# A graph layer in fp32: the convolution's weights as a ring of nine single taps, more lead in the first group, fewer turns of the identity

## The chip, the cores and the metric

The kernel runs on one core of a Trainium2 chip. The metric is the device time of one execution in microseconds; three executions of the kernel before are given with their median. The profile is that of one more execution, taken by the hardware profiler. The engines are TensorE (PE: matmuls; PEld: its weight loads, which lie beside them), VectorE (DVE), ScalarE (ACT), GpSimd (POOL) and SyncE (SP, which issues most of the DMAs).

## The reference, cut to what matters

Inputs: `x` (32, 512, 256) and a 0/1 matrix `adj` (32, 512, 512), all in fp32, with the weights of one layer. Cut down, the reference is

```python
h = maximum(layernorm(x), 0)
# 1: two convolutions along the 512 positions, 1 tap and 17 taps, 256 -> 256 channels
c = relu(bn1(conv1d(h, conv1_w)))
x_conv = relu(bn2(conv1d(c, conv2_w, pad=8)) + h)
# 2: messages over the graph
s = h @ w_se.T + b_se                                  # 3 numbers a node
A = exp(-squared_distance(s, s)) * adj
x_nmp = A @ relu(h @ w_msg.T + b_msg)
# 3: a gated unit
gi = concat(x_conv, x_nmp) @ w_ih.T + b_ih
gh = h @ w_hh.T + b_hh
r, z = sigmoid(gi_r + gh_r), sigmoid(gi_z + gh_z)
n = tanh(gi_n + r * gh_n)
out = x + (1 - z) * n + z * h
```

## The kernel before, in words

**The 17-tap convolution** is the part that the change touches. It is done by a fast algorithm with two nested levels of five evaluation points: 25 products of transformed weights with transformed inputs take the place of the direct sum of taps. The 32 batches are laid end to end and cut into 7 groups (`STARTS`, L36), since one group's input is what the memory holds. So there are 7 x 25 = 175 products, numbered m = 25 g + n. Each product has an operand `x2` (made on VectorE from the first convolution's output `h1`, by `fives`, `operands` and `operand_some`, L432 to L492 and L741) and a weight `w` with two or three parts, here called taps, of `[128, 2, 256]` each (index k of `w[:, k]`, L524). A product with n = 6 (`LONE`) uses tap 1 alone.

In the **first group** (g = 0) the weights are made on the chip: `weights_first` (L527) combines rows of `wraw` on VectorE into `gg`, ScalarE scales them into `w` (two activations of 512 columns, L558) and issues one DMA that puts both taps into DRAM (`WD`, L562). `prepare_some` (L757) runs this generator piece by piece, never further than three weights beyond the product in work. A product of this group is two halves on TensorE, each of 16 matmul instructions of 116 columns, which read taps 0 and 1.

From the **second group** on the weights are read back: `weights_again` (L567) takes a buffer and issues one DMA on SP for all taps of one product. In the second group tap 2 is the sum of taps 0 and 1, made on VectorE (`third_weight`, L577) and also put into DRAM; later groups read all three. A product then is: tap 2 with `x2[1]` into PSUM, a copy of the result by ScalarE, then taps 0 and 1 with the differences `xd` (L843 to L849). Weights have 3 buffers of three taps, `x2` has 6 buffers. `AHEAD` (L726) limits how many operands are made beyond the product in work: one more than its value.

**The order of all work is planned by the program itself** when it is built. Five streams (rows, begins, graphs, conv, gates; L1336) are Python generators. A planner (L1383) holds a clock `now` of TensorE's time, made of estimates for each instruction (`matmul`, `turn`, and the `Engine` class for VectorE and ScalarE), and at each turn of its loop lets the stream that is furthest behind its share emit its next piece. Every engine works its own instructions strictly in the order in which they were emitted. Where a stream yields a time, it isn't asked again before that time; where it yields a function, it waits until that is true. Between the pieces `fill` and `background` (L1260) emit VectorE's and ScalarE's work that nobody waits for yet: layer norms, operands, weights, sums; weights and operands of the next two products go first.

If no stream is ready, the planner adds 0.25 us to `now` and tries again (L1386). From the third such round in a row on it emits, on each round, **two turns of the identity** on TensorE (`keep_warm`, L143): transposes into a PSUM tile that nobody reads (`unused`, named `ps_acc`). They don't move `now`. This ends as soon as the first gate's input is asked for (`HB`), which is after all 25 weights are made, near the end of the first group. Another 16 such turns stand at the start (L1349).

`load_graph` (tile `hTg`), `load_gates` (`hTb`), `load_sums` (`xnb`) and the masks (`m_sb`, in `Graphs.ask`) are DMAs on SP's queue, as are the weights that are read back; `hT` and `x_sb` are loaded there too.

Of the kernel before, what the change touches and what calls it, by code (L numbers as in the profile page):

```python
# [49 lines left out]
def kernel(  # L50
# [434 lines left out]
    def operands(g):  # L485

        rv = sizes(g)[3]
        h = h1[:, : Q * rv].rearrange("p (q e) -> p q e", q=Q)
        for x1 in fives(h, 6, rv, lambda: phases("x1", 6, rv, 2), again=True):
            yield None  # L490
            if x1 is not None:
                yield from fives(x1, 2, rv, lambda: phases("x2", 2, rv, 6))  # L492
# [30 lines left out]

    def new_w():  # L524
        return cv.tile([P, 3, ND, D], F32, name="w", bufs=3)

    def weights_first():  # L527
# [10 lines left out]
        for j1 in ORDER:  # L538
# [12 lines left out]
            for j2 in ORDER:  # L551
# [5 lines left out]
                w = new_w()  # L557
                for i in range(ND):  # L558
                    act.activation(
                        w[:, :2, i, :], gg[i], AF.Copy, scale=GSCALE[j1] * GSCALE[j2]  # L560
                    )
                nc.scalar.dma_start(WD[len(WS)][:, :2], w[:, :2])  # L562
# [4 lines left out]
    def weights_again(m):  # L567

        w = new_w()
        k = slice(1, 2) if m % 25 == LONE else slice(0, 2 if m < 50 else 3)  # L570
        nc.sync.dma_start(w[:, k], WD[m % 25][:, k])
        WS.append(w)
        W_AT.append(now + 7.0)
# [3 lines left out]
    def third_weight(m):  # L577
        if m in thirds or m % 25 == LONE:
            return
        thirds.add(m)  # L580
        w = WS[m]
        dve.tensor_tensor(w[:, 2], w[:, 0], w[:, 1], op=ALU.add)
        later(dve.free + 0.4, lambda: nc.gpsimd.dma_start(WD[m % 25][:, 2], w[:, 2]))
        W_AT[m] = dve.free + LAG
# [141 lines left out]
    AHEAD = 3  # L726
# [31 lines left out]
    def prepare_some():  # L758
        nonlocal prepare_at
        if len(WS) >= 25 or len(WS) >= at_product + 3 or now < prepare_at:  # L760
            return False
# [3 lines left out]
    def convolution():  # L765
# [3 lines left out]
        def product(ps, *terms, clear=(True, True)):  # L769


            for o in range(ND):
                pairs = [
                    (w[:, k, i, o * P : (o + 1) * P], t[:, at + i * (nu + 1) : at + i * (nu + 1) + nu])
# [19 lines left out]
        for g in range(NG):  # L794
# [9 lines left out]
            for n in range(25):  # L804
# [3 lines left out]
                while 25 <= len(WS) < min(m + 2, 25 * NG):  # L808
                    weights_again(len(WS))
# [26 lines left out]
                else:  # L836
# [5 lines left out]
                    else:  # L842
# [3 lines left out]
                        if 25 <= len(WS) == m + 2 < 25 * NG:  # L846
                            weights_again(m + 2)
# [8 lines left out]
                if 25 <= len(WS) == m + 2 < 25 * NG:  # L856
                    weights_again(m + 2)
# [525 lines left out]
    while streams:  # L1383
        names = [k for k in streams if hold[k] is None or hold[k]()]
        able = [k for k in names if ready[k] <= now]
        if not able:  # L1386
# [3 lines left out]
            if waits > 2 and not HB:  # L1390
                keep_warm(2)
# [67 lines left out]
```

## Time and profile before

| | us |
|---|---|
| median of three runs | 2068.64 (2067.52 to 2070.0) |
| the profiled execution | 2070.59 |
| its span, first to last instruction | 2068.8 |
| first products of the second convolution start | 57.5 |
| the first group's last product ends | 231.5 |
| first gate matmuls | 247.3 |

The parts of the page used below are the busy time of each engine with its share of the span and its instructions, and the clock granted to TensorE in 40 slices, in tenths of full speed. A table by stretches gives, for each, its length, then the busy time of PE, PEld, DVE, ACT and POOL with the number of instructions, the mean clock, the share of time that the DMA engines were busy, and GB/s. A line of time gives the start and the length of an instruction (or of several alike in a row), engine, line, operation, output and input by name, form and count; in brackets stands the idle time of the engine ahead of it, and what ended it. Nearly all instructions carry the line of the helper that emitted them: L136 (matmul), L141 (turn), L146 (turn of the identity), L127 (VectorE and ScalarE), so one goes by the names of the tiles. In the first group `ps_c<-x,w` are the products of the second convolution, `ps_g<-ident,m_sb` the masks' turns, `ps_g<-at,msg` the sums over the graph, `w<-gg` the scaling of weights, `x<-x` the operands.

### The profile page before, as it was taken

What the parts mean: (1) busy time and instruction counts of PE and PEld (TensorE: products, weight loads), DVE (VectorE), ACT (ScalarE), POOL (GpSimd) and SP (SyncE); (2) the same over time, 40 slices, a digit from 0 to 9 for tenths busy, and PEclk for the clock granted to TensorE, in tenths of its full rate; (3) what the DMA queues carried; (4) which work ended last, traced back from release to release, by engine and by line L of the source; (5) the groups of instructions that cost most, each with busy time, mean ns of one, the idle gap of its engine ahead of it and who ended that gap; (6) DMA issues with size and microseconds to landing.
All of it is one profiled execution on the core that took longest, in us unless ns stands there. A gap on an engine that the chain in (4) does not pass through costs nothing.

```text
span 2068.8 us, 25327 instructions
## 1 busy us (share of the span) xinstructions
PE 2046.3 (99%) x8724; PEld 1256.4 (61%) x8724; DVE 1319.8 (64%) x2378; ACT 827.0 (40%) x1585; POOL 451.7 (22%) x578
## 2 busy tenths in 40 slices
PE   9999999999999999999999999999999999999998
PEld 5888566666666666665666665566665666644444
DVE  5789677865877667775677663667766576532223
ACT  6544553343543446234353333533344433342221
POOL 2101122321312113221132212322211211132222
PEclk9999999999999999999999999999999999999999
DMA  7455768887889768986799876978776777555554
GB/s 274 162 173 194 250 202 224 190 216 200 193 243 208 195 187 227 211 198 177 189 214 219 188 197 155 227 192 193 171 206 176 184 176 158 148 113 91 68 92 36
DMA packets 539312, 378.31 MB, mean 183 GB/s; under 512 B 452992, under 2 KB 470432, under 8 KB 538048
## 3 DMA queue, kind: packets, MB, share of 16 engines
q1 hardware_dynamic: 381312, 278.74, 47.9%
q0 software_dynamic: 153184, 84.70, 23.9%
q10 hardware_dynamic: 4688, 13.24, 1.7%
q8 instruction: 70, 1.15, 0.2%
q14 instruction: 58, 0.48, 0.1%
HBM read 278.55 MB, written 114.56 MB: 190 GB/s over the span
## 4 chain that ended last, share of the span: by engine, by line
PE 61%; DVE 1%; issue 1%; DMA 0%; POOL 0%; ACT 0%; DVEq 0%; POOLq 0%; ACTq 0%
PE ps_acc L136 36%; PE ps_c L136 13%; PE ps_g L136 10%; PE ps_c L917 1%; PE ps_g L141 0%; DMA cd<-part 0%; DVE y L127 0%; POOL cd L721 0%; DVE part L127 0%; ACT part L127 0%; DVE o_sb L127 0%; DVE right L127 0%; DVE x L127 0%; POOL out_dram L1146 0%; PE ps_g L917 0%
## 5 line engine op out<-in xcount | busy, mean ns | idle before, releaser
L1146 POOL DMA_DIRECT2D out_dram<-o_sb x252 | 276.6, 1733 | 522.1 <-DVE o_sb L127 512.6
L136 PE MATMUL ps_acc<-xconv,wih 128*128 128x512 f32 (+1 forms) x772 | 361.3, 590 | 0.0
L136 PE MATMUL ps_acc<-xnb,wih 128*128 128x512 f32 (+1 forms) x772 | 360.4, 592 | 0.0
L136 PE MATMUL ps_acc<-hTb,whh 128*128 128x512 f32 (+1 forms) x772 | 356.1, 590 | 0.0
L136 PEld LDWEIGHTS ps_c<-xd,w 128*128 128x128 f32 x2304 | 288.6, 191 | 65.2 <-issue 56.2
L136 PEld LDWEIGHTS ps_c<-x,w 128*128 128x128 f32 x2032 | 256.1, 191 | 82.9 <-issue 66.2
L136 PE MATMUL ps_c<-xd,w 128*128 128x135 f32 (+1 forms) x2304 | 291.9, 280 | 0.7 <-ACT ps_c L127 0.4
L136 PE MATMUL ps_c<-x,w 128*128 128x135 f32 (+2 forms) x2032 | 265.3, 279 | 3.1 <-ACT n L127 1.7
L136 PE MATMUL ps_g<-at,msg 128*128 128x512 f32 x512 | 227.0, 593 | 1.3 <-DVE at L127 1.3
L136 PEld LDWEIGHTS ps_acc<-xnb,wih 128*128 128x128 f32 x772 | 141.4, 191 | 140.8 <-issue 137.5
L136 PEld LDWEIGHTS ps_acc<-xconv,wih 128*128 128x128 f32 x772 | 140.7, 190 | 141.6 <-issue 139.7
L136 PEld LDWEIGHTS ps_acc<-hTb,whh 128*128 128x128 f32 x772 | 140.5, 190 | 138.9 <-issue 136.9
L127 DVE TENSOR_TENSOR o_sb<-hTb,r 128x512 f32<-128x512 f32 x63 | 43.4, 689 | 215.6 <-ACT r L127 215.5
L127 DVE TENSOR_TENSOR msg<-ps_g,bmsg 128x256 f32<-128x256 f32 x128 | 54.0, 422 | 190.5 <-PE ps_g L136 190.4
L136 PEld LDWEIGHTS ps_g<-at,msg 128*128 128x128 f32 x512 | 95.0, 190 | 109.4 <-issue 103.8
L127 DVE SCALAR_TENSOR_TENSOR x<-x,x 128x544 f32<-128x544 f32 (+5 forms) x161 | 137.6, 854 | 2.7
L127 DVE TENSOR_TENSOR xd<-x 128x544 f32<-128x544 f32 (+1 forms) x144 | 102.5, 717 | 42.4 <-PE ps_c L136 42.3
L127 DVE TENSOR_TENSOR x<-x 128x272 f32<-128x272 f32 (+5 forms) x280 | 127.1, 498 | 0.3
L136 PE MATMUL ps_g<-wmsg,hTg 128*128 128x259 f32 x496 | 122.3, 381 | 0.0
L136 PE MATMUL ps_g<-hT,w 128*128 128x512 f32 (+8 forms) x296 | 117.6, 545 | 0.0
L127 ACT ACTIVATE ps_c<-ps_c 128x270 f32<-128x270 f32 (+1 forms) x144 | 56.6, 393 | 150.6 <-PE ps_c L136 150.5
L127 ACT ACTIVATE z<-ps_acc,brz 128x512 f32<-128x512 f32 x64 | 43.9, 686 | 179.0 <-PE ps_acc L136 179.0
(124 smaller groups left out, 2354.2 us busy)
## 6 DMA issues: line engine op xcount, KB each, us to landing
w<-wd SPq DMA_DIRECT2D x120, 768.0 KB, 5.6
m_sb<-in_adj_dram SPq DMA_DIRECT2D x384, 64.0 KB, 3.9
hT<-hd SPq DMA_DIRECT2D x33, 512.0 KB, 4.4
hd<-hT POOLq DMA_DIRECT2D x32, 512.0 KB, 6.4
hTb<-hd SPq DMA_DIRECT2D x32, 512.0 KB, 5.3
xnb<-nd SPq DMA_DIRECT2D x64, 256.0 KB, 3.1
out_dram<-o_sb POOLq DMA_DIRECT2D x252, 64.0 KB, 5.0
hTg<-hd SPq DMA_DIRECT2D x31, 512.0 KB, 4.5
```

The costliest lines, as they stand in the source:

```text
L127: getattr(self.engine, name)(*tiles, **more)
L136: nc.tensor.matmul(ps, lhsT, rhs, **more)
L917: nc.tensor.matmul(pss[c], gr.left[k, :], gr.right[k, :], start=True, stop=True, tile_position=(32 * c, 0),)
L1146: nc.gpsimd.dma_start(dst, src, accum_op=ALU.add)
```

## The change

Four edits go together.

1. A weight buffer holds one tap instead of three, and there are nine of them instead of three (the same memory). In the first group two taps are taken per product; each is scaled by two activations of 256 columns and put into DRAM by a DMA of its own. In later groups `weights_again` becomes one generator over all products that takes and loads tap by tap, in the order in which the product uses them (2, 0, 1). `load_weights` runs it until nine taps beyond those done are asked for: at the start of a product, and once more behind its first third. The calls at the end of a product are dropped.
2. `AHEAD` is 4 instead of 3, and `x2` has 7 buffers instead of 6.
3. Weights of the first group may be made five beyond the product in work instead of three.
4. While no stream is ready, one turn of the identity is emitted on rounds 3, 7, 11 and so on of the wait, instead of two on each round from the third.

```diff
--- before.py
+++ after.py
@@ -489,7 +489,7 @@
         for x1 in fives(h, 6, rv, lambda: phases("x1", 6, rv, 2), again=True):
             yield None
             if x1 is not None:
-                yield from fives(x1, 2, rv, lambda: phases("x2", 2, rv, 6))
+                yield from fives(x1, 2, rv, lambda: phases("x2", 2, rv, 7))
 
     def ends(x2, rv):
 
@@ -521,8 +521,13 @@
 
     WS, W_AT = [], []
 
+    RING = 9
+    W_BASE, taken = [], 0
+
     def new_w():
-        return cv.tile([P, 3, ND, D], F32, name="w", bufs=3)
+        nonlocal taken
+        taken += 1
+        return cv.tile([P, ND, D], F32, name="w", bufs=RING)
 
     def weights_first():
 
@@ -554,23 +559,38 @@
                     gg.append(next(inner[i]))
                     yield 0.0
                 yield dve.free + 0.1
-                w = new_w()
-                for i in range(ND):
-                    act.activation(
-                        w[:, :2, i, :], gg[i], AF.Copy, scale=GSCALE[j1] * GSCALE[j2]
-                    )
-                nc.scalar.dma_start(WD[len(WS)][:, :2], w[:, :2])
+                W_BASE.append(taken)
+                w = [new_w(), new_w()]
+                for k in range(2):
+                    for i in range(ND):
+                        act.activation(
+                            w[k][:, i, :], gg[i][:, k, :], AF.Copy, scale=GSCALE[j1] * GSCALE[j2]
+                        )
+                    nc.scalar.dma_start(WD[len(WS)][:, k], w[k])
                 WS.append(w)
                 W_AT.append(act.free + LAG)
                 yield 0.0
 
-    def weights_again(m):
-
-        w = new_w()
-        k = slice(1, 2) if m % 25 == LONE else slice(0, 2 if m < 50 else 3)
-        nc.sync.dma_start(w[:, k], WD[m % 25][:, k])
-        WS.append(w)
-        W_AT.append(now + 7.0)
+    def weights_again():
+        for m in range(25, 25 * NG):
+            W_BASE.append(taken)
+            w = {}
+            for k in (1,) if m % 25 == LONE else (2, 0, 1):
+                yield
+                w[k] = new_w()
+                if k < 2 or m >= 50:
+                    nc.sync.dma_start(w[k], WD[m % 25][:, k])
+            WS.append(w)
+            W_AT.append(now + 7.0)
+
+    again = weights_again()
+
+    def load_weights(done):
+
+        while len(WS) >= 25 and taken < done + RING and next(again, 0) is None:
+            pass
 
     thirds = set()
 
@@ -579,8 +599,8 @@
             return
         thirds.add(m)
         w = WS[m]
-        dve.tensor_tensor(w[:, 2], w[:, 0], w[:, 1], op=ALU.add)
-        later(dve.free + 0.4, lambda: nc.gpsimd.dma_start(WD[m % 25][:, 2], w[:, 2]))
+        dve.tensor_tensor(w[2], w[0], w[1], op=ALU.add)
+        later(dve.free + 0.4, lambda: nc.gpsimd.dma_start(WD[m % 25][:, 2], w[2]))
         W_AT[m] = dve.free + LAG
 
     SUMS = []
@@ -723,7 +743,7 @@
             evacuated[b] = PARTS[-1]
         return True
 
-    AHEAD = 3
+    AHEAD = 4
     HB_AT, gating = {}, 0
     XC, XC_AT, RES, evacuated = {}, {}, {}, {}
     X2, X_AT, XD = [], [], {}
@@ -757,7 +777,7 @@
 
     def prepare_some():
         nonlocal prepare_at
-        if len(WS) >= 25 or len(WS) >= at_product + 3 or now < prepare_at:
+        if len(WS) >= 25 or len(WS) >= at_product + 5 or now < prepare_at:
             return False
         prepare_at = next(prepare)
         return True
@@ -771,7 +791,7 @@
 
             for o in range(ND):
                 pairs = [
-                    (w[:, k, i, o * P : (o + 1) * P], t[:, at + i * (nu + 1) : at + i * (nu + 1) + nu])
+                    (w[k][:, i, o * P : (o + 1) * P], t[:, at + i * (nu + 1) : at + i * (nu + 1) + nu])
                     for k, t, at in terms
                     for i in range(ND)
                 ]
@@ -805,8 +825,7 @@
                 at_product = m = 25 * g + n
                 if n == 6:
                     yield lambda: not EVAC
-                while 25 <= len(WS) < min(m + 2, 25 * NG):
-                    weights_again(len(WS))
+                load_weights(W_BASE[m] if m < len(W_BASE) else taken)
                 if m == 24:
                     yield lambda: len(WS) >= 25
                 if late is None and len(WS) >= 25:
@@ -843,8 +862,7 @@
                         product(ps[0], (2, x2[:, 1, :], 0), clear=(True, False))
                         act.activation(ps[1], ps[0], AF.Copy)
                         yield act.free + LAG
-                        if 25 <= len(WS) == m + 2 < 25 * NG:
-                            weights_again(m + 2)
+                        load_weights(W_BASE[m] + 1)
                         for k in range(2):
                             product(ps[k], (k, XD[m][:, k, :], 0), clear=(False, False))
                         del XD[m]
@@ -853,8 +871,6 @@
                 if g > 0:
                     later(now + 0.3, hand)
                 at_product = m + 1
-                if 25 <= len(WS) == m + 2 < 25 * NG:
-                    weights_again(m + 2)
                 yield now
                 if g > 0:
                     yield lambda: done is None
@@ -1387,8 +1403,8 @@
             now += 0.25
             assert now < 1e4
             waits += 1
-            if waits > 2 and not HB:
-                keep_warm(2)
+            if waits % 4 == 3 and not HB:
+                keep_warm(1)
             fill()
             continue
         name = min(able, key=lambda k: clock[k])
```

## The prediction

> **What bounds the kernel now.** I read the busy shares first, then the granted clock and the busy time by stage, then the waits of TensorE, and last TensorE's line of time through the first group, looking for turns of the identity (the tile they write is `ps_acc`, at L146).
>
> ```profile
> PE 2046.3 (99%) x8724; PEld 1256.4 (61%) x8724; DVE 1319.8 (64%) x2378; ACT 827.0 (40%) x1585; POOL 451.7 (22%) x578
> PEclk9999999999999999999999999999999999999999
> ```
>
> TensorE is the bound, but "busy" counts the turns too: L146 has 142 of them. By stage (span of the stretch, then PE, PEld, DVE, ACT and POOL busy, clock, DMA share, GB/s):
>
> ```profile
> 20.00:40.00 20.00, 18.56 (x70) 10.49 (x69) 8.71 (x13) 12.45 (x28) 2.12 (x3) 0.83 0.72 274
> 60.00:80.00 20.00, 19.09 (x169) 17.98 (x169) 18.96 (x38) 14.15 (x28) 3.56 (x4) 1.00 0.45 144
> 80.00:100.00 20.00, 19.67 (x114) 14.43 (x114) 11.51 (x36) 6.68 (x13) 2.37 (x3) 1.00 0.55 206
> 100.00:120.00 20.00, 20.00 (x147) 17.13 (x147) 15.90 (x26) 15.01 (x25) 1.12 (x2) 1.00 0.56 184
> 160.00:180.00 20.00, 19.48 (x163) 18.05 (x162) 19.32 (x47) 12.39 (x24) 2.09 (x2) 1.00 0.50 178
> ```
>
> Here the reader sees that VectorE is nearly full in one stretch (18.96 of 20) and half idle in the next (11.51), while TensorE works on. From 270 us to the end TensorE has only 3.8 us of idle time that the profile names (its waits there: ACT h 1.3, ACT n 1.1, ACT z 1.0, ACT ps_c 0.4). So nothing but the work of TensorE counts there, and all that can be saved lies before 270 us. One piece of it, from TensorE's line of time and, below it, from those of ScalarE and VectorE:
>
> ```profile
> 103.44 0.60 PE L141 MATMUL ps_g<-ident,m_sb 128*128 128x128 f32 x4
> 103.88 1.47 PE L146 MATMUL ps_acc<-ident 128*128 128x128 f32 x12
> 105.19 0.60 PE L141 MATMUL ps_g<-ident,m_sb 128*128 128x128 f32 x4
> 105.63 1.91 PE L146 MATMUL ps_acc<-ident 128*128 128x128 f32 x16
> 107.37 0.60 PE L141 MATMUL ps_g<-ident,m_sb 128*128 128x128 f32 x4
> 107.81 0.38 PE L146 MATMUL ps_acc<-ident 128*128 128x128 f32 x2
> 108.03 1.94 PE L136 MATMUL ps_c<-x,w 128*128 128x116 f32 x16
> ...
> 106.89 1.15 ACT L127 ACTIVATE w<-gg 128x512 f32<-128x512 f32 x2
> 89.91 0.43 DVE L127 TENSOR_TENSOR msg<-ps_g,bmsg 128x256 f32<-128x256 f32 x1 [6.91 <-PE ps_g L136]
> ```
>
> The product at 108.03 takes the weights that ScalarE ended at 106.89 + 1.15 = 108.04. In the 4.6 us before it TensorE did 1.3 us of mask turns and 30 turns of the identity. And from 83.0 to 89.91 VectorE stood idle for 6.91 us, when it could have prepared those weights: the list then held 8 of them at product 5, which is the old limit (product plus 3).
>
> **What the Trainium skill says.** "Perfetto Trace Analysis", section "Identifying the Most-Contended Engine", says that the busy share of matmuls is a bad measure of what TensorE has left. The trace agrees: the 99% holds 142 turns that compute nothing. "TensorE: Matmul & The Clock Gate", section "What's actually happening": an idle window of about 3.4 us halves the clock, a busy one brings it back. The trace agrees: the clock was 0.50 from about 30.3 to 37.2 us and from 259.4 to 266.0, each behind a stretch with few matmuls. The same page, "Part 4: PE-mode transpose", says that transposes don't count as busy in the same way. The trace doesn't decide it: ten turns at 31.82 did not end a half-clock stretch, yet from 17.8 to 23.2 us nothing but turns ran and the clock stayed 1.00.
>
> **Fewer turns.** The start-up 16 stay. The other 126 came as 2 for each turn of the waiting loop from the third on; a burst of n means n/2 + 2 rounds of 0.25 us in the planner. The new rule gives one at rounds 3, 7, 11. For the 18 bursts of the trace, waits unchanged, that is 23 instead of 126. One costs (105.19 - 103.88) / 12 = 0.109 us at full clock, 0.219 at half (31.82 to 34.01, ten). So at most 103 x 0.109 = 11.2 us goes, but only where the next instruction could have started sooner. Up to 57 us I compared each burst with the end of what its successor reads. Bursts at 1.83, 9.08, 17.79, 39.53 and 45.92 lie in real waits (hT ends at 9.92 and the first convolution starts at 9.95): worth nothing. At 21.93 hT had ended at 21.86: 1.31 us less two turns that stay, 1.1. At 31.82 hT had ended at 30.08: 2.19 us less two at half clock, 1.75. Together 2.85. Against it: if the turns held the clock, the stretch from 17.8 to 22 goes to half speed, and one such stretch costs half of 6.9, or 3.4 us. Bounds 0 and 3.4; I take 1.0, because only a part of that stretch loses its turns (8 of 13). Net **1.9 us**.
>
> **Operands and weights further ahead** (weights 3 to 5 beyond the product, operands 3 to 4, one x2 buffer more). At stake from 57 to 232 us are 68 turns, 7.4 us, and 2.5 us of named idle time. Ahead of products stand: 0.22 at 70.86; 3.28 at 103.88 to 108.03 (12 + 16 + 2 turns); 0.87 at 146.71; 0.87 at 165.63; 1.1 and 0.52 (waits for DVE x) at 175.99 to 178.20; 0.22 at 203.35: 7.1 us. The rest is other people's: 0.65 + 0.28 at 136.21 and 0.33 at 99.78 (ACT n, a PSUM bank), 0.22 + 0.45 at 214.56 (ACT right), 0.91 at 75.24 (DVE at); I count 0.4 of their turns. No instruction is added on VectorE, only moved, into gaps such as 83 to 90 and 116 to 122.6. VectorE is busy 131.7 of 160 us between 60 and 220 (the eight stretches added), so 87% of a stage that is 9 us shorter: it fits on the whole, not everywhere. I take three quarters: 0.75 x 7.1 + 0.4 = **5.7 us**. Both ends: 0.4 (VectorE is late next) and 7.9. In later groups the same limit moves operands only; TensorE waited for DVE x nowhere after 232 us, so nothing.
>
> **Single taps in the first group.** Each of 25 weights now takes four activations of 256 columns and two DMA issues on ScalarE, instead of two of 512 and one. A 512-wide one took 0.629 us, a 270-wide one 0.395: 256 columns are some 0.38, so 4 x 0.38 - 2 x 0.629 = 0.26 us more. The issue waits for the activation ahead of it, 0.40 us of idle ScalarE in the trace (49.12 to 49.53); one more per weight. 0.66 x 25 = 16.5 us on ScalarE, which is busy 81 of 160 us there. Behind it in the queue stand the evacuations of ps_c and the exponentials, for which TensorE waited 1.1 us in this stage. Bounds 0 and 16.5 (no reason for a gain); I take **0.8 us lost**.
>
> **Single taps later.** The ring holds the same 9 taps as 3 x 3 before. Reloads on SP grow from 24 + 1 + 125 = 150 to 24 x 2 + 1 + 5 x (24 x 3 + 1) = 414, and an issue took 0.37 us (214.63): 98 us more on SP in 1800 us, a queue that mostly waits (w alone stood 325 us behind ps_c). A tap is asked for as soon as the product that frees it is issued, so SP stands until TensorE gets there; behind it wait masks, hTg, hTb and xnb loads. A step lasts (2068 - 232) / 150 = 12.2 us and a load landed in 5.6, and TensorE never waited for a DMA: cover enough. Zero taken. Without the cover: a mask or graph load late by 1 us in each of 28 graphs, through VectorE, 28 us at worst; below, zero, as there is no wait to win.
>
> **The change of group** (232 to 270 us: 4.3 us idle, and half of 6.6 us at half clock, 3.3) isn't touched but is dealt anew: between 3 us better and 3 worse; zero taken.
>
> **The sum** against the profiled execution: 1.9 + 5.7 - 0.8 = 6.8; 2070.59 - 6.8 = 2063.8 us (its span is 2068.8, 1.8 us lie around it). It lies 1.95 above the median of the three runs; against that, 2068.64 - 6.8 = **2061.8 us**. About 0.2%, or 4.1 us, is what a measurement of this kernel can tell from no change: 2064.5 and 2072.8 are the bounds.
>
> **Rivals.** (1) The forecast: waits ahead of products go. For it: the gap of 6.91 us on VectorE stands just ahead of the longest wait. (2) The wait moves: VectorE (18.96 and 19.32 of 20 us) or ScalarE is late next, and only the useless turns go: 1.9 + 0.4 + a tenth of 7.1 - 0.8 = 2.2, so 2066.4. For it: those two stretches. Against it: the empty ones beside them. (3) The turns held the clock. Place: the thin stretches up to 57 us, then around 103 to 108 and 165 to 178 if waits stay. Price 3.4 us for each half-clock stretch beyond the two of before. It decides from two such stretches on (6.8 us are gone), and makes the kernel slower by over 0.2% at four: 2061.8 + 4 x 3.4 = 2075.4. For it: 0.50 at 30.3 shows how little is needed. Against it: after 57 us the products are dense, and fewer waits mean fewer thin stretches. (4) SP's queue makes masks late: 1 us in half the graphs, 14 us, about 2076; against it stands the 12.2 us step.
>
> **How the numbers follow.** (1) 0.62, nearly all of it faster by over 0.2%; (2) 0.25, within it; (3) 0.08 and (4) 0.05, slower. Faster 0.62, same 0.25, slower 0.13. The range: everything won is 2.85 + 7.9 + 3 = 13.8, or 2054.9, less 1.1 for the spread of the runs (2067.52 was the lowest), 2053.8; upward it takes in (2) with a change of group 3 us worse (2069.4) and half of (3) and (4), 2073. Below and above I leave some 0.06 and 0.11.
>
> **What would show it.** Right: some 10 to 35 turns in L146 in place of 142; no burst between two mask turns near 103; the last product of the first group ends some 7 us sooner than 231.5; TensorE's named waits past 270 us still about 4 us; the clock in the first 57 us with one half-speed stretch. Wrong: waits "PE ps_c <- DVE x" or "<- ACT w" of over 4 us ahead of 232 us (rival 2); more than two stretches at 0.50 (3); "DMA m_sb" or "DMA hTg" as a releaser of VectorE or TensorE (4).

## The result, and the profile after

| | before | after |
|---|---|---|
| median (range), us | 2068.89 (2065.53 to 2071.07), 6 runs | 2076.79 (2075.23 to 2078.22), 6 runs |
| ratio to before, with 95% interval | | 1.0038 [1.0027, 1.0049] |
| the profiled execution, its span | 2070.59, 2068.8 | 2077.32, 2075.6 |
| turns of the identity | 142 | 40 |
| first group's last product ends | 231.7 | 233.4 |

The change makes the kernel 7.9 us slower, where 6.8 us faster was forecast. (By the trace the first group ended at 231.7 us before, a little later than the 231.5 given ahead.) The lines of the page that answer to those of before:

```profile
PE 2041.6 (98%) x8622; PEld 1249.4 (60%) x8622; DVE 1321.6 (64%) x2378; ACT 836.7 (40%) x1635; POOL 451.8 (22%) x578
...
w<-wd SPq DMA_DIRECT2D x414, 256.0 KB, 3.5
```

TensorE has 102 instructions fewer and is busy 4.7 us less, yet the span is 6.7 us longer: what was added are waits. ScalarE has 50 activations more, and the weights come back in 414 loads, as counted. The row of the granted clock is all nines again. L146 alone (durations in ns, lowest, median and highest):

```profile
L146 PE MATMUL ps_acc<-ident x40: 271/420/477, 1.8 to 184.7; 128*128 128x128 f32 x40
```

The stretches shown of before, now in the kernel after (columns as there), and one more:

```profile
20.00:40.00 20.00, 18.50 (x60) 9.89 (x61) 10.66 (x15) 13.69 (x31) 2.38 (x4) 0.83 0.74 278
60.00:80.00 20.00, 19.43 (x172) 18.30 (x171) 16.93 (x33) 14.67 (x34) 1.89 (x2) 1.00 0.45 161
80.00:100.00 20.00, 18.14 (x99) 13.66 (x99) 16.15 (x40) 9.62 (x18) 2.35 (x4) 0.99 0.52 184
100.00:120.00 20.00, 19.10 (x156) 17.99 (x155) 13.70 (x26) 12.87 (x33) 0.60 (x1) 0.93 0.36 119
160.00:180.00 20.00, 19.95 (x118) 15.48 (x117) 17.09 (x39) 8.01 (x18) 2.76 (x12) 1.00 0.38 131
260.00:280.00 20.00, 13.79 (x83) 11.74 (x82) 15.65 (x23) 16.85 (x29) 3.50 (x6) 0.83 0.56 197
```

VectorE's work lies more evenly, as the longer leads should make it (18.96 and 11.51 became 16.93 and 16.15). The new thing is the last line: from 260 to 280 us TensorE is busy 13.79 of 20 us. The burst of turns ahead of a product near 103 is gone too; TensorE's line of time there:

```profile
107.82 5.62 PE L136 MATMUL ps_c<-x,w 128*128 128x116 f32 x48
113.27 0.60 PE L141 MATMUL ps_g<-ident,m_sb 128*128 128x128 f32 x4
```

Three half products (48 matmuls) run without a gap. So the leads and the turns do what was said of them, and the time is lost elsewhere. Two larger stretches, before and then after:

```profile
57.00:234.00 177.00, 173.80 (x1195) 142.80 (x1193) 138.22 (x285) 90.84 (x176) 16.43 (x30) 1.00 0.56 192
234.00:300.00 66.00, 62.17 (x278) 42.20 (x279) 52.87 (x109) 30.70 (x58) 12.56 (x19) 0.95 0.72 227
```

```profile
57.00:234.00 177.00, 169.33 (x1121) 136.83 (x1119) 132.23 (x271) 95.32 (x215) 17.09 (x30) 0.99 0.54 182
234.00:300.00 66.00, 56.63 (x255) 39.18 (x256) 50.03 (x94) 28.84 (x52) 9.94 (x17) 0.92 0.76 240
```

From these traces I made one table. Each TensorE instruction counts from its start to the start of the next, less the idle time that the profile names ahead of the next. Turns are counted whole. Of everything else, half of what lies at half clock is booked as clock loss (the time ahead of the first record of full clock counts as such), and what remains is "work" (waits too short to be named are in it). The idle time before the first instruction and the end behind the last matmul are left out. Microseconds, before to after:

| stretch (cut at 57.4) | work | turns | named idle | clock loss |
|---|---|---|---|---|
| 0 to 57 | 38.4 to 38.3 | 11.7 to 6.2 | 3.3 to 6.3 | 2.3 to 4.7 |
| 57 to 234 | 165.5 to 166.4 | 7.8 to 1.0 | 3.6 to 7.6 | 0 to 1.7 |
| 234 to 300 | 59.4 to 52.0 | 0 to 0 | 3.5 to 9.2 | 2.9 to 4.9 |
| whole span | 2018.4 to 2021.5 | 19.4 to 7.2 | 14.1 to 26.0 | 8.6 to 13.1 |

Of the 6.8 us of turns that leave the first group, 0.9 becomes work; 4.0 becomes idle time and 1.7 half clock. Then, at the change of group, 7.4 us less work is done in the same 66 us. Over the whole span the turns give 12.2 back, idle time takes 11.9, the clock 4.5, and work 3.1 more: 7.3 us lost, beside a span longer by 6.7. TensorE's waits from 234 to 300 us (total, times, longest), before and then after:

```profile
PE ps_c L917 <- ACT n L127: 1.8, 1, 1.8
PE ps_g L141 <- ACT at L127: 1.4, 1, 1.4
PE ps_g L136 <- DVE at L127: 0.8, 1, 0.8
```

```profile
PE ps_c L136 <- ACT z L127: 5.2, 2, 4.9
PE ps_g L136 <- DVE at L127: 3.0, 1, 3.0
```

These are the two costliest of the kernel after there. In both, TensorE waits for an engine that does the right thing too late in its queue. ScalarE and then TensorE of the kernel after, around the longest:

```profile
267.19 5.46 ACT L127 ACTIVATE xconv<-y,bn_shift,bn_scale 128x504 f32<-128x504 f32 x8
272.56 1.07 ACT L127 ACTIVATE x_sb<-x_sb,shift,rstd 128x256 f32<-128x256 f32 x2
273.54 0.65 ACT L127 ACTIVATE z<-ps_c 128x272 f32<-128x272 f32 x2
...
273.96 2.18 PE L136 MATMUL ps_c<-x,w 128*128 128x136 f32 x8 [4.89 <-ACT z L127]
```

The evacuation (the copy out of TensorE's accumulators, PSUM, that frees the bank for the next product; here `z<-ps_c`) stands behind eight writes of `xconv`, 5.46 us, and two scalings of `x_sb`, 1.07 us, and TensorE waits 4.89 us for the bank. In the kernel before, four such writes ran from 253.02 ahead of an evacuation, and the wait was 1.82 us. VectorE at the other long wait, and TensorE below it:

```profile
238.89 0.63 DVE L127 SCALAR_TENSOR_TENSOR z<-n 128x464 f32<-128x464 f32 x1
239.56 1.61 DVE L127 TENSOR_TENSOR y<-y,z 128x1392 f32<-128x1392 f32 x1
241.08 0.68 DVE L127 TENSOR_TENSOR at<-ps_g,at 128x512 f32<-128x512 f32 x1
...
241.82 3.63 PE L136 MATMUL ps_g<-at,msg 128*128 128x512 f32 x5 [3.03 <-DVE at L127]
```

The last mask's turn ended at 238.79; its multiplication on VectorE (`at`) stood behind two sums of the second convolution (0.63 + 1.61 us).

### The profile page after: what moved, and what is told of

Same layout as the page of the kernel before. It is cut to its first block, busy times and chain, and to the rows that moved or that the text cites. A ratio compares the mean times of both kernels' runs of the same rounds, so it can differ in the third digit from the quotient of the medians.

```text
span 2075.6 us, 25795 instructions
## 1 busy us (share of the span) xinstructions
PE 2041.6 (98%) x8622; PEld 1249.4 (60%) x8622; DVE 1321.6 (64%) x2378; ACT 836.7 (40%) x1635; POOL 451.8 (22%) x578
## 4 chain that ended last, share of the span: by engine, by line
PE 92%; DVE 3%; ACT 2%; DMA 1%; issue 1%; SPq 0%; ACTq 0%; POOL 0%; DVEq 0%; POOLq 0%
PE ps_acc L136 46%; PE ps_c L136 22%; PE ps_g L136 20%; PE ps_g L141 1%; PE ps_c L933 1%; ACT x_sb L127 0%; DVE x L127 0%; DVE z L127 0%; DVE gg L127 0%; DMA xd<-x_sb 0%; DVE at L127 0%; DMA xconv<-cd 0%; ACT w L127 0%; PE ps_g L933 0%; ACT y L127 0%
```

## The experiments

The theories that the expectations name: **A**, the loss is a worse order at the change of group, from the longer leads; **B**, the removed turns held the clock; **C**, single taps cost ScalarE (or SP) in the first group, and **C'**, the split loads cost SP later; **D**, the planner deals the order anew and the deal makes the loss, whatever part sets it off; **E**, evacuations of PSUM banks stand behind work that the planner takes for free; **F**, the ring itself costs. "Order kept" means that TensorE, VectorE and GpSimd have the same instructions in the same order as the base, row by row. Medians of the kernel before beside these runs were 2069.41, 2069.75, 2066.61 and 2069.21 us; "over before" and ratios are to the one of the same runs. Differences are of medians; the ratios, which are given with their 95% intervals, differ from them by up to 2.2 us.

**The new rule for turns alone**, in the kernel before; order kept but for the turns.

```diff
-            if waits > 2 and not HB:
-                keep_warm(2)
+            if waits % 4 == 3 and not HB:
+                keep_warm(1)
```

> The kernel before with the rule for the turns of the identity alone changed; the order of all other work is the same. Theory A (the loss is in the new order of work at the change from the first group to the second, 232 to 300 us, that the longer leads bring about): 2064 to 2069 us; some 100 turns go, part of them turns into idle time and one more half-clock stretch, and 232 to 300 us look as before. Theory B (the turns held the clock): 2073 us or more, with at least two half-clock stretches more than the three of before. Theory C (single taps cost ScalarE and SP more): as A.

Measured: 2064.47 us, 0.9981 [0.9973, 0.9989], 39 turns. This edit alone wins 4.9 us; B falls as the cause of the loss.

**The reverse**, the kernel after with the old rule (the four lines above turned round). Only TensorE's turns differ from the kernel after.

> The changed kernel with the old rule for the turns: ring and leads alone. A: 2075 to 2081 us, since the waits at the change of group stay (idle time of TensorE from 234 to 300 us of 8 us or more). B: 2070 us or less. C: as A.

Measured: 2078.36 us, 1.0046 [1.0028, 1.0065]. The turns are worth 1.6 us in the new order, within these intervals nothing. The loss is in the rest.

**No longer leads** (kernel after), and **the ring alone** (this, with the old rule for turns too).

```diff
-                yield from fives(x1, 2, rv, lambda: phases("x2", 2, rv, 7))
+                yield from fives(x1, 2, rv, lambda: phases("x2", 2, rv, 6))
...
-    AHEAD = 4
+    AHEAD = 3
...
-        if len(WS) >= 25 or len(WS) >= at_product + 5 or now < prepare_at:
+        if len(WS) >= 25 or len(WS) >= at_product + 3 or now < prepare_at:
```

> The changed kernel with the old leads (AHEAD 3, six x2 buffers, weights three beyond the product): ring and fewer turns alone. A: 2064 to 2070 us, like fewer turns alone. B: 2073 us or more, like fewer turns alone. C: 2074 us or more, and clearly above fewer turns alone.

> The kernel before with the ring of nine single taps alone (old leads, old turns). A: 2067 to 2071 us. B: the same. C: 2073 us or more, with waits of TensorE for ACT w or for a DMA.

Measured: 2093.9 us, 1.0119 [1.0098, 1.0139], and 2093.7 us, 1.0118 [1.0098, 1.0138]. A falls so far as it blames the leads: without them it is 17 us worse, not better. The ring alone comes out 24 us slower than before. Its largest wait, from its trace (TensorE, VectorE and ScalarE):

```profile
722.83 0.71 DVE L127 STREAM_TRANSPOSE hT<-x_sb 128x512 f32<-128x512 f32 x1 [8.54 <-PE ps_g L136]
...
724.04 3.61 DVE L127 TENSOR_TENSOR y<-y,z 128x1632 f32<-128x1632 f32 x2
...
731.45 0.69 ACT L127 ACTIVATE z<-ps_c 128x272 f32<-128x272 f32 x2 [15.64 <-DVE y L127]
...
731.90 2.18 PE L136 MATMUL ps_c<-x,w 128*128 128x136 f32 x8 [9.11 <-ACT z L127]
```

VectorE stood 8.54 us for a buffer, the sums of `y` came late behind it, ScalarE's evacuation waited for those, and TensorE 9.11 us for the bank. No weight and no load of weights is in this chain: it is an order that fits badly.

**ScalarE's part of the single taps alone**, in the kernel before, the planner told the old durations; order kept.

```diff
-                    act.activation(
-                        w[:, :2, i, :], gg[i], AF.Copy, scale=GSCALE[j1] * GSCALE[j2]
-                    )
-                nc.scalar.dma_start(WD[len(WS)][:, :2], w[:, :2])
+                    act.free = max(act.free, now) + act.fixed + act.each * 2 * D
+                for k in range(2):
+                    for i in range(ND):
+                        nc.scalar.activation(
+                            w[:, k, i, :], gg[i][:, k, :], AF.Copy, scale=GSCALE[j1] * GSCALE[j2]
+                        )
+                    nc.scalar.dma_start(WD[len(WS)][:, k], w[:, k])
```

> The kernel before, order of all work kept to the instruction, but each first-group weight made as the change makes it: four activations of 256 columns and two DMA issues on ScalarE, some 0.66 us more of ScalarE for each of 25. Theory C (ScalarE's extra work is the cost of the single taps): 2074 us or more, with waits of TensorE for ACT w, z and n of over 5 us ahead of 234 us. Theory D (what the parts cost is a new deal of the order, not their own work): 2068 to 2071 us.

Measured: 2072.68 us, 1.0017 [1.0007, 1.0027]: 3.3 us, not 0.8. From its waits of ScalarE between 57 and 234 us:

```profile
ACT w L562 <- ACT w L562: 8.9, 22, 0.5
```

ScalarE stands 8.9 us behind its own activations with the next weight at hand, since each store waits for the result that it stores; no such line is among its waits in the kernel before. The cost lies between C's range (2074 us or more) and D's (2071 or less).

**Another deal of the order.** The planner's share for the graphs is changed by 1%; nothing that is computed, no buffer and no limit changes. In the kernel before:

```diff
-        "graphs": (all_graphs(), 11.5 * PER, -0.5),
+        "graphs": (all_graphs(), 11.6 * PER, -0.5),
```

> The kernel before with one planner constant moved by 1% (the graphs' share, 11.5 to 11.6), which orders most of the work anew and changes no buffer, no lead, no instruction of the products. Theory D: off from before by more than 4 us, either way, with other waits at the changes of group. Theory C: 2067 to 2071 us.

Measured: 2082.81 us, 1.0074 [1.0058, 1.0089]: 13.4 us lost by the order alone. Its longest wait of TensorE (ScalarE, then TensorE):

```profile
262.55 0.69 ACT L127 ACTIVATE n<-ps_c 128x272 f32<-128x272 f32 x2 [5.60 <-DVE z L127]
...
263.29 0.95 PE L917 MATMUL ps_c<-right,left 5*128 5x512 f32 x1 [4.84 <-ACT n L127]
```

It is a wait of the same size as in the kernel after and at the same change of group, for another evacuation (`n`). It is a part of the 13.4 us only: over the whole trace TensorE's named waits come to 24 us, where the kernel before has 14 (without the first, ahead of all work).

**The same in the kernel after** (11.6 there).

> The changed kernel with the same planner constant moved by 1%. D: off from the changed kernel by more than 4 us, either way. C: 2074 to 2079 us.

Measured: 2075.64 us, 1.0036 [1.0022, 1.0049]. No move that can be told, where D had said more than 4 us, though 4246 of TensorE's 8582 instructions other than turns fall out of the common sequence when the two traces are compared: a new deal need not cost or win.

**Stores of the first group's weights from GpSimd** in the kernel after, 0.4 us behind the activations by the planner's clock. VectorE's and TensorE's order kept.

```diff
-                    nc.scalar.dma_start(WD[len(WS)][:, k], w[k])
+                    later(act.free + 0.4, lambda d=WD[len(WS)][:, k], s=w[k]: nc.gpsimd.dma_start(d, s))
```

> The changed kernel, order kept, with the first group's stores of taps issued by GpSimd instead of ScalarE, so that ScalarE neither waits for its own activation nor issues there. C: 2070 us or less. D: 2073 to 2078 us, since the order stays.

Measured: 2070.37 us, 1.0011 [1.0003, 1.0020]: 6.4 us faster than the kernel after (5.6 by the ratios), against D, which had said 2073 us or more. This is the largest single cost that was found in it. Its profiled execution took 2076.11 us, the highest of 22, but since TensorE's order is that of the kernel after, the two traces can be laid side by side. The last products of the first group and the first gate, in the kernel after and then with GpSimd's stores:

```profile
229.56 3.83 PE L136 MATMUL ps_c<-x,w 128*128 128x116 f32 x32
...
253.99 1.88 PE L136 MATMUL ps_acc<-hTb,whh 128*128 128x512 f32 x4
```

```profile
222.34 3.83 PE L136 MATMUL ps_c<-x,w 128*128 128x116 f32 x32
...
248.08 1.88 PE L136 MATMUL ps_acc<-hTb,whh 128*128 128x512 f32 x4
```

| us | before | turns alone | after | after, GpSimd's stores |
|---|---|---|---|---|
| first products start | 57.5 | 54.3 | 57.3 | 57.0 |
| first group's last product ends | 231.7 | 227.6 | 233.4 | 226.2 |
| first gate matmuls | 247.3 | 243.2 | 254.0 | 248.1 |
| span | 2068.8 | 2061.0 | 2075.6 | 2074.3 |

So the gain lies in the first group: its last product ends 7.2 us sooner, and TensorE's named waits from 57 to 234 us fall from 7.4 to 4.3 us. The change of group stays bad. From the end of the last product to the first gate the old order takes 15.6 us in both of its traces here, the new one 20.6 and 21.9: there are eight turns of masks more, about 1 us, and the rest is waits and half clock. The two waits named above stand in the trace with GpSimd's stores too: 3.2 us for `at` ahead of the first gate, 4.5 us for `z` behind it.

**Loads by tap**, in the kernel before: three DMAs of 256 KB in place of one of 768, at the old moments; order kept.

```diff
-        nc.sync.dma_start(w[:, k], WD[m % 25][:, k])
+        for one in ((1,) if m % 25 == LONE else (0, 1) if m < 50 else (2, 0, 1)):
+            nc.sync.dma_start(w[:, one], WD[m % 25][:, one])
```

> The kernel before, order of all engines kept, but each weight that is read back comes by one DMA per tap (three issues on SP for one, as with the ring, at the old moments and into the old three buffers). Theory C' (the split loads and SP's queue cost the later groups): 2074 us or more. Theory D (only the new deal of the order costs there): 2068 to 2071 us.

Measured: 2068.75 us, 0.9997 [0.9986, 1.0008]. C' falls for the old buffers and moments; the forecast's zero was right there.

**A planner that sees two of ScalarE's waits**: the kernel with GpSimd's stores, with ScalarE's planned clock put behind VectorE's ahead of the evacuations to `n` and `z`, and 0.7 us more for each write of `xconv`.

```diff
             sum_all(read)
+            act.behind(dve)
...
             settle()
+            act.behind(dve)
...
+            act.free += 0.7
             if o == ND - 1:
-                evacuated[b] = XC_AT[b] = act.free + 0.7 + LAG
+                evacuated[b] = XC_AT[b] = act.free + LAG
```

> The changed kernel with stores of taps on GpSimd (as after_stores_pool) and a planner that counts two things that it left out: that ScalarE waits for VectorE's sums before it empties a bank into z or n, and 0.7 us more for each evacuation of the first two batches. Theory E (the loss at the change of group comes from bank evacuations that stand on ScalarE behind work which the planner takes for free): the wait of 4.5 to 5 us near 270 us goes, 2062 to 2068 us. Theory D (any deal may be good or bad): anything from 2060 to 2090 us, with waits of over 4 us elsewhere.

Measured: 2073.64 us, 1.0025 [1.0015, 1.0035], slower than its base. TensorE's waits from 234 to 300 us begin with

```profile
PE ps_g L136 <- DVE at L127: 2.7, 1, 2.7
PE ps_c L136 <- ACT z L127: 2.4, 1, 2.4
```

so the wait aimed at (4.5 us in the base) is halved, and in the traces 60.7 us of work is done there where the base did 53.2. But most of that is clock: the base's trace has three half-clock stretches there, a loss of some 6.4 us, and this one has none. And this too is a new deal: past 300 us its named idle time is 9.4 us against 4.2, a wait of 4.54 us for a reload of `hT` at 720 among it, and the total is worse. The total lies above E's range (2062 to 2068 us). E says why a wait is there, and not what removing it is worth.

**GpSimd's stores with the new turns** in the kernel before (one store a weight, as there):

```diff
-                nc.scalar.dma_start(WD[len(WS)][:, :2], w[:, :2])
+                later(act.free + 0.4, lambda d=WD[len(WS)][:, :2], s=w[:, :2]: nc.gpsimd.dma_start(d, s))
```

> The kernel before with the new rule for turns, and the first group's weight stores issued by GpSimd; three-tap buffers, old leads, order of TensorE and VectorE kept. If ScalarE's store waits count on the path (theory C in the first group): 2060 to 2063 us. If they are covered there: 2063 to 2066 us, like fewer turns alone.

Measured: 2064.78 us, 0.9980 [0.9972, 0.9989], the same as the turns alone. In its trace the first group's last product ends at 225.8 us, 1.8 sooner than with the turns alone, but the total doesn't show it. One store a weight costs little or nothing in the old order; whether it is the second store or the other order that makes the 6.4 us of the kernel after isn't separated.

**Operands further ahead alone**, in the kernel before (`AHEAD` 4, `x2` with 7 buffers).

```diff
-                yield from fives(x1, 2, rv, lambda: phases("x2", 2, rv, 6))
+                yield from fives(x1, 2, rv, lambda: phases("x2", 2, rv, 7))
...
-    AHEAD = 3
+    AHEAD = 4
```

> The kernel before with AHEAD 4 and seven x2 buffers alone. If one more operand of lead is worth what the forecast said of waits ahead of products (its part of 5.7 us): 2063 to 2068 us. Theory D: as likely slower than faster, 2060 to 2090 us, decided by the waits at the changes of group and not by those ahead of 234 us.

Measured: 2069.65 us, 1.0006 [0.9995, 1.0018]: nothing, in an order that differs much (3956 of TensorE's 8582 instructions fall out of the common sequence).

**Weights further ahead alone**, in the kernel after (the same two places set back, five weights kept).

```diff
-                yield from fives(x1, 2, rv, lambda: phases("x2", 2, rv, 7))
+                yield from fives(x1, 2, rv, lambda: phases("x2", 2, rv, 6))
...
-    AHEAD = 4
+    AHEAD = 3
```

> The changed kernel with the old lead of operands (AHEAD 3, six x2 buffers): ring, fewer turns and the weights' lead of five. If the weights' lead wins the 17 us: 2074 to 2080 us. If the operands' lead does: 2090 us or more, as without both.

Measured: 2088.5 us, 1.0108 [1.0095, 1.0122]. That is 21.9 us over before, in neither range and nearer to the second: of the 24.5 us that the ring with the new turns costs, 2.6 come back with the weights' lead, and 14 more with the operands'. In the kernel before, the operands' lead was worth nothing: the parts don't add up.

**The ring in the old order**: the ring alone, but loads at the old moments and the planner told the old durations; TensorE, VectorE and GpSimd then do exactly the kernel before.

```diff
-        return cv.tile([P, ND, D], F32, name="w", bufs=RING)
+        return cv.tile([P, ND, D], F32, name="w", bufs=9)
...
+                for i in range(ND):
+                    act.free = max(act.free, now) + act.fixed + act.each * 2 * D
...
-                        act.activation(
+                        nc.scalar.activation(
...
-                load_weights(W_BASE[m] if m < len(W_BASE) else taken)
+                while 25 <= len(WS) < min(m + 2, 25 * NG):
+                    weights_again(len(WS))
...
```

> The ring of nine single taps with its split activations, stores and loads, but the planner's clock fed with the old durations and moments, so that TensorE, VectorE and GpSimd do the same work in the same order as before. Theory D (the ring's 24 us are the new order of work): 2070 to 2074 us, as for the split activations alone. Theory F (the ring itself costs): 2085 us or more.

Measured: 2070.91 us, 1.0023 [1.0011, 1.0034], or 4.3 us beside 2066.61. This is the run that decides between D and F: of the 24 us of the ring alone, some 4 (2 to 7 by the interval) are the ring's own, of the size of ScalarE's part (3.3), and 20 go with the order and, set back together with it, the moments of the loads.

**Two more deals**: the ring alone with 11.6, and the kernel before with 11.4.

```diff
-        "graphs": (all_graphs(), 11.5 * PER, -0.5),
+        "graphs": (all_graphs(), 11.6 * PER, -0.5),
```

> The ring alone with the planner's share of the graphs at 11.6 instead of 11.5. D: off from the ring alone (2093.7 us) by more than 5 us, most likely lower, 2070 to 2088 us. F: 2090 to 2097 us.

> The kernel before with the planner's share of the graphs at 11.4. D: 2070 to 2090 us, above before, as at 11.6 (2082.8 us). If before is no good deal but an ordinary one: within 4 us of it.

Measured: 2075.35 us, 1.0044 [1.0030, 1.0057], so 8.7 us over before where the ring alone was 24.3; and 2086.95 us, 1.0102 [1.0088, 1.0116], 20.3 us over before. In the latter the largest wait of TensorE, 3.6 us, is for `ps_c` at 1046.0, behind a write of `part` on ScalarE that had stood 5.50 us for a DMA. A part of a deal's price is clock: the runs' mean granted clock was 0.992 in the ring alone and in the deal with 11.4, and 0.995 and 0.996 in the kernel before beside them. 0.004 of 2070 us is some 8 us, by my estimate, of the 24.3 and of the 20.3.

**Turns and the clock.** The turns alone with 30 turns at the start in place of 16, and the kernel before with those 16 and none later.

```diff
-    keep_warm(16)
+    keep_warm(30)
```

```diff
-            if waits > 2 and not HB:
-                keep_warm(2)
```

> The kernel before with the new rule for turns, but 30 turns at the start instead of 16 (before, 30 came in one burst there). If the shorter start burst leaves the clock at half for longer (until about 10.5 us in the changed kernel, 6.4 before): 2060 to 2063 us, below fewer turns alone. If not: like fewer turns alone, 0.19% under before.

> The kernel before with the 16 turns of the start and none later, order kept. Turns without effect on the clock (theory A[...]): at or up to 2 us below fewer turns alone, so 0.2 to 0.3% under before. Turns hold the clock (theory B): at or above before, with two or more further half-clock stretches ahead of 234 us.

Measured: 2065.46 us, 0.9985 [0.9976, 0.9995], and 2065.32 us, 0.9992 [0.9982, 1.0002], against 2064.47 with the new rule: three rules, no difference that can be told. The trace without later turns has full clock through the first group:

```profile
57.00:234.00 177.00, 168.10 (x1107) 134.17 (x1106) 139.44 (x273) 90.82 (x175) 16.02 (x30) 1.00 0.58 199
```

**The version that beats both kernels** is the first of these runs, the turns alone: 2064.47 us, 4.9 us under the kernel before and some 12 under the kernel after.

## Why the prediction was wrong, step by step

**What bounds the kernel.** "Nothing but the work of TensorE counts there" (from 270 us on) was drawn from the small waits of one order. They were small because of that order: the ring alone has a wait of 9.11 us at 731.9, the redealt kernel before one of 3.55 at 1046. The kernel after has one of 4.89 at 273.96, more than the 4 us in all that were to show past 270; past 300 us its named idle time is 2.9. And waits weren't all that could be lost there: the kernel before's own trace has a third half-clock stretch, from 464.0 to 470.8 us, where the prediction speaks of two. A list of small waits describes an order and doesn't bear a forecast for another.

**Fewer turns**: predicted 1.9 us, measured 4.9 (2.3 to 5.6 from the interval). The mechanism was right and the size too small by a factor of 2.6. Instruction by instruction, the traces show the two bursts that were priced: TensorE gains 1.1 us behind the one at 21.93 and 1.75 behind the one at 31.82, exactly as forecast. The clock risk of 1.0 that was subtracted came in this trace as one half-clock stretch more, from 8.0 to 11.5 us, but TensorE met a wait of 0.67 us for VectorE (`shift`, 16.84 in the kernel before) that took up what it had lost. So the first products start 3.2 us sooner (54.3), and another 0.9 us is won in the first group, where the forecast counted bursts under another heading. 40 turns are left in the kernel after; the prediction's own sum was 16 + 23, though its list of signs said 10 to 35.

**Operands and weights further ahead**: predicted 5.7 us. The mechanism was right: the burst near 103 is gone, VectorE's work is even, and with the turns as before the kernel with leads has done 164.7 us of work between 57 and 234, the ring alone 159.5. These 5.2 us are not shown to be the leads' own work, since the order differs too. Against the kernel before only 0.9 is left of it (the first table). With the stores on GpSimd the first group's last product ends 5.5 us sooner than before (226.2 against 231.7), where some 7 were forecast: in the first group the forecast is nearly met once the stores are out of the way.

**Single taps in the first group**: predicted 0.8 us lost, measured 3.3 (ScalarE's edits alone) to 4.3 (the ring whole) in the old order, and 6.4 came back in the new one when GpSimd issued the stores. What they cost ScalarE was right: a weight takes 2.28 us where it took 1.57, so 0.71 each, predicted 0.66. ScalarE of the kernel after, at one weight:

```profile
43.90 0.72 ACT L127 ACTIVATE w<-gg 128x256 f32<-128x256 f32 x2
44.65 0.35 ACTq L569 DMA_DIRECT2D wd<-w  x1
45.05 0.72 ACT L127 ACTIVATE w<-gg 128x256 f32<-128x256 f32 x2 [0.43 <-ACT w L127]
...
46.18 0.72 ACT L127 ACTIVATE w<-g 128x256 f32<-128x256 f32 x2 [0.41 <-ACT w L127]
```

The error is in what lies on the path. I took ScalarE's mean busy share (half) as cover; but evacuations and exponentials queue strictly behind the weights, and a delay there can pass through a bank to TensorE. The pair of traces with and without ScalarE's stores shows some of it: from 57 to 234 us TensorE's waits for `at` (0.9 us on VectorE, 0.6 on ScalarE) and `aug` (0.7) are gone, those for `z` fall from 2.3 to 1.4 and those for `w` itself from 0.8 to 0.2, while those for `n` stay (1.9 and 2.2). The half-clock stretch from 99.5 to 102.9 us is gone too. The Trainium skill, "DMA: Bandwidth & Descriptors", section "Issuing engines are not separate DMA queues", says that DMAs on several engines save only the sequencer's time to issue, usually small beside the transfer. The trace agrees on the size (0.33 to 0.35 us an issue), and the kernel after with its stores on GpSimd (6.4 us) shows that on an engine that others wait for the issue, with the 0.4 us of waiting ahead of it, can count.

**Single taps later**: predicted 0, measured 0 (loads by tap). No wait of TensorE in the kernel after names a DMA, with 414 loads where 150 were counted before.

**The change of group, "dealt anew: between 3 us better and 3 worse; zero taken"** is the step that failed. The planner's order is a function of every estimate and limit in the program, so the change deals not one seam but everything anew: by a comparison of the two traces, 4435 of TensorE's 8582 instructions other than turns and 1953 of VectorE's 2378 fall out of the common sequence. What a deal is worth was measured with nothing else changed: +13.4 and +20.3 us in the kernel before, -15.6 in the ring alone, -1 in the kernel after (and about 0 with operands ahead, where a limit changes too). So the bounds had to be some 15 to 20 us wide and not 3. In the kernel before both deals lost: it is the best by 13 us of the three of its own program that were run, which makes a new one likelier to lose than to win, if three deals can say so. In the change itself the seam takes 5.0 us more up to the first gates (20.6 in place of 15.6, 1 us of it work that moved there), where zero was taken.

**The sum.** Turns and the single taps' own work, measured one by one in the old order, make -4.9 + 4.3 = -0.6 us; with the figures of the new order -1.6 + 6.4 = +4.8. The whole is +7.9. So 3 to 8.5 us are left for leads and order together, where the forecast had -5.7: they miss it by 9 to 14 us. Of the whole miss of 14.7 us, with the figures of the new order, 8.8 fall on leads and order, 5.6 on the single taps (6.4 in place of 0.8), which are the second step that failed, and 0.3 on the turns. That the order can do this is shown; that its share lies at 234 to 300 us, where the kernel after does 7.4 us less work, is what the traces with this order say, and no run takes that seam away alone. The one that aimed at it changed the whole order. Why the leads win back 17 us from the ring alone, and nothing in the kernel before, stays open.

**The rivals.** (2), the wait moves, comes nearest: idle time took 11.9 of the 12.2 us of turns, but the late engine was late because of its queue's order and not because it was full (16.93 and 17.09 of 20 us), and mostly at 234 to 300 us and not ahead of products. (3), the turns held the clock: the trace shows its sign, more than two half-clock stretches, and yet it is wrong as the cause of the loss, as the turns alone and the kernel with no later turns show; the clock still takes 4.5 us more in the kernel after. (4), SP makes masks late: its sign didn't come, as no wait of VectorE or TensorE there names the masks or `hTg`. The chance for slower, 0.13, came from (3) and (4) alone; the cause that did it was not among the cases.

## What to carry to other kernels

Where a planner orders the work of engines that keep to that order, a change of an estimate, a buffer count or a limit can deal the whole order anew: before forecasting, see what a neutral 1% change of one share does (here -16 to +20 us), and take that as the range. To know what a part costs by itself, keep the order (feed the planner the old numbers) and change only the part. And judge a slowdown of a half-busy engine by what stands behind it in its queue, not by its mean share.

## What was not expected of the hardware

Half-clock stretches came in lengths of 3.4 and 6.8 us (one of 10.2 in the ring alone) and differ between executions in which TensorE has the same instructions in the same order: the kernel before had one from 464.0 to 470.8 us, the ring in the old order none there. From 460 to 475 us, before and then the ring in the old order (the last three columns: clock, DMA share, GB/s):

```profile
460.00:475.00 15.00, 13.79 (x45) 7.27 (x44) 2.71 (x5) 7.96 (x18) 1.31 (x2) 0.77 0.58 204
```

```profile
460.00:475.00 15.00, 13.79 (x53) 7.10 (x52) 5.38 (x9) 8.53 (x20) 1.90 (x3) 1.00 0.67 216
```

Both were busy 13.79 us; one ran at 0.77 and one at 1.00. Over the whole span the stretches cost 8.6 us in the one and 4.4 in the other. The Trainium skill, "TensorE: Matmul & The Clock Gate", section "What's actually happening", says that the window of the clock gate is free-running, so that where it lies against the program varies; the traces agree in that the same order meets different stretches. With the idle window of about 3.4 us that the prediction quotes from the same section the traces agree less well than it says: in the 8 us ahead of the three half-clock stretches of the kernel before TensorE was busy for 7.67, 5.60 and 6.79 us, much of it turns and short matmuls, and never idle for 3.4 us on end. What the gate counts as idle isn't shown here. Most of the scatter of the runs goes with the granted clock: of the 27 runs of the kernel before beside the first experiments the fastest, 2062.69 us, had a mean granted clock of 0.998 and the slowest, 2075.18 us, one of 0.993; over all of them time and clock are correlated at -0.94.

Full clock came first at 6.6 us in the kernel before, at 10.8 after and at 13.8 with no later turns, and the total did not show it (2065.32 us with none later, 2065.46 with 30 at the start).
